# Layer 2's strips: one tile column of 64 rows a turn in place of 16 rows by 32 columns

## The chip, the cores and the metric

The kernel runs on one core of one Trainium2 chip. The metric is the device time of one execution in microseconds (us). TensorE (PE, with PEld for its weight loads), VectorE (DVE), ScalarE (ACT) and GpSimd (POOL) compute; SyncE (SP) issues every transfer between the chip's memory (HBM) and the on-chip memory. All arithmetic is in f32.

## The reference, cut to what matters

Sixteen images of 64 x 64 tokens with 256 channels pass through four residual layers, each fed by a group normalisation:

```
x = x + attention(gn(x))          # layer 0
x = x + gated_scan(gn(x))         # layer 1, ends in a batch norm over all images
x = x + involution3(gn(x))        # layer 2, 3x3 kernels made from x
x = x + involution7(gn(x))        # layer 3, 7x7 kernels made from x
```

The change concerns how the output of layer 2 reaches layer 3. Layer 3 multiplies 7x7 patches by weights that differ from token to token. Its patches are of the normalised tensor, so the mean of each channel's group is taken off first ("centred"); the scale is applied later. Tokens outside the image count as zero after centring.

## The kernel before, in words

**Three stages.** The first does layer 0 and the maps of layer 1 (to about 3420 us, layer 1's scan in it), the second (here stage B) the end of layer 1 and layer 2, the third (stage C, from about 6090 us) layer 3.

**Stage B** (from L899) is a loop over 152 turns, its order written by hand. An image has eight chunks of 512 tokens; in a turn the loop runs four jobs on chunks of different images, behind each other by the `LAG` of L1184. `end_of_layer1` (lag 0) makes `x2` from `x1` and the factors `pf`: DVE's two operations at L975, ACT, then POOL's two additions at L985. `projected` (lag 13) is PE and ACT work. The 3x3 involution (lag 21) is the DVE's heavy part: two products at L1107 of 4608 elements a partition and one sum at L1276; the other sum is made on POOL (L1120 in three steps, L1121), which DVE adds to at L1228. `turned` transposes the result `x3` (written as `x3_d`, token-major) to `c3` (written as `c3_d`, channel-major), and `norm3` finds the group means after an image's last chunk. `centred` (lag 32) is the job that the diff touches: it takes 512 tokens of `x3_d` into a tile `xc`, POOL subtracts the means at L880 into `cen`, and `cen` is written to the DRAM tensor `strips`.

**The tensor `strips`** is `[image, 4 quarters of 64 channels, 64 + 9 rows, 8 + 6 columns, 8 tile columns, 64 channels]`. Stage C works on tiles of 3 rows by 8 columns with a border of 3, so the 64 columns are kept as eight tile columns of 14, side by side; columns near a tile's edge are stored twice, once for its neighbour. A token's position inside the tile is u (0 to 7), its tile column t (0 to 7). For u from 5 to 7 there is a second copy for the next tile column, for u from 0 to 2 one for the previous.

**The job before:** job `rc` takes 16 rows (`part`) and half of the tile columns (`th`), so 16 x 32 tokens, by four loads with u slowest on the 128 partitions (p = 16 u + r). It writes, for each of the four quarters, three transfers: all eight u, then the two borders of three u each: 12 transfers.

**The transfers** all stand in SP's program, so SP's queue has this order in a turn: loads of the next turn (`x2p`, `x2r`, `x1` twice, `pf` twice), then the stores collected in the turn before (`x2`, the 12 strips, `x3` twice, `c3` twice), then the four loads of `xc`: 27 transfers. L942 is the line of the loads, L1213 that of the stores, L1281 that of the stores left at the end.

**The last image** is centred in stage C. Stage C has 704 turns `n` (16 images, 4 quarters, 11 pairs of tile rows). Each loads two sets of patches for the turn n + 4 (`xw`, L1413), every second one the residual (`rx`, L1433) and an output store (L1527); every third loads `c3` for the turn n + 2 (L1313), from which the next image's 7x7 weights start with the matmul at L1346. PE makes weight matrices (L1379) and applies them (L1445). Eight times, at turns n = 44 k + 1, `xc` is loaded (L1521), POOL centres in the turn after, and the 12 stores follow four a turn (L1523). `xc` and `cen` use two of the six buffers of `xw` here.

Of the kernel before, what the change touches and what calls it, by code (L numbers as in the profile page):

```python
# [15 lines left out]
P = 128  # L16
C = 256
HW = 64
# [10 lines left out]
TR, TC = 3, 8  # L29
NTR, NTC = 22, HW // TC  # L30
# [6 lines left out]
def network(ctx: ExitStack, tc: tile.TileContext, a: dict, out: bass.AP):  # L37
    nc = tc.nc
    NI = a["x"].shape[0]
# [45 lines left out]
    x3_d = dram.tile([NI, NT, C], F32, tag="x3_d", name="x3_d")  # L85
    c3_d = dram.tile([NI, P, 2, NT], F32, tag="c3_d", name="c3_d")
    strips = dram.tile([NI, 4, HW + 9, TC + 6, NTC, 64], F32, tag="strips", name="strips")
# [92 lines left out]
    with ExitStack() as st:  # L180
# [12 lines left out]
        for v in (wo[:, 0], wo[:, 1], bout):  # L193
            mean = small.tile([P, 1], F32, tag="wmean", name="wmean")
# [20 lines left out]
        def load(kind, i, ch):  # L215

            tag = {"xin": "xin", "xn": "xn"}.get(kind, "x1")
            t = wk.tile([P, 2, CT], F32, tag=tag, name=kind, bufs=4 if tag == "x1" else 2)
            src = a["x"][i, ch]
            if kind == "xm":  # L220
                src = x1_d[i, :, :, ch * CT : (ch + 1) * CT].rearrange("h p t -> p h t")
            nc.sync.dma_start(out=t, in_=src)
            loaded[kind, i, ch] = t
# [293 lines left out]
        def jobs(n):  # L517
            m, t = divmod(n, NCH)
            i, hf = divmod(m, 2)
            d = n - LAST  # L520

            def at(k):
                return 0 <= k < NI

            todo = []
            if at(i):
                todo.append(("q", i, hf, t))
            if hf == 0:
                if at(i + 1):
                    todo.append(("xin", i + 1, t))  # L530
            elif at(i - 1) and d < 0:
                todo.append(("x1", i - 1, t))
            if 6 <= d < 10:
                todo += [("x1", NI - 1, 2 * d - 12 + k) for k in range(2)]

            if at(i - 2) and (t >= 2 if hf == 0 else t < 2):
                todo.append(("xm", i - 2, (t - 2) % NCH))
            if 12 <= d < 16:
                todo += [("xm", NI - 1, 2 * d - 24 + k) for k in range(2)]
            return todo  # L540
# [24 lines left out]
        for n in range(LAST + 16):  # L565
            m, t = divmod(n, NCH)
# [64 lines left out]
    with ExitStack() as st:  # L631
# [24 lines left out]
        with tc.tile_pool(name="s_conv", bufs=1) as pcv:  # L656
# [4 lines left out]
                out=lsa.rearrange("p i j c -> p (i j c)"), in_=a["lsa_w"].partition_broadcast(P)  # L661
# [27 lines left out]
        for n in range(10):  # L689
            delta, c = n // 2, n % 2  # L690
# [28 lines left out]
        with tc.manual_schedule():  # L719
            steps = [(ch, g) for ch in range(NCH) for g in range(NG)]  # L720
            rows, ins, hsts = {}, {}, {}
# [23 lines left out]
            for n, (ch, g) in enumerate(steps):  # L745
# [18 lines left out]
                b, k = g * 8, min(8, NI - g * 8)  # L764
# [8 lines left out]
        n = NI * NCH  # L773
# [94 lines left out]
            )  # L868
        return lambda: nc.vector.tensor_copy(dst, pb[:, 0:C])

    def centred_from(i, rc):

        part, th = divmod(rc, 2)
        x3n = x3_d[i].rearrange("(r t u) c -> u r t c", t=NTC, u=TC)
        return [x3n[:, part * 16 : part * 16 + 16, th * 4 + t, :] for t in range(4)]

    def centred_strips(i, rc, xc, cen, mean):

        part, th = divmod(rc, 2)
        nc.gpsimd.tensor_tensor(  # L880
            cen.rearrange("p q t c -> p t q c"),
            xc.rearrange("p t (q c) -> p t q c", q=4),
            mean.rearrange("p (q c) -> p q c", q=4).unsqueeze(1).broadcast_to([P, 4, 4, 64]),
            ALU.subtract,
        )
        parts = []
        rows = slice(3 + 16 * part, 19 + 16 * part)
        for q in range(4):
            for u0, u1, w0, dt in ((0, TC, 3, 0), (TC - 3, TC, 0, 1), (0, 3, TC + 3, -1)):
                t0, t1 = max(0, th * 4 + dt), min(NTC, th * 4 + 4 + dt)  # L890
                s0 = t0 - th * 4 - dt
                parts.append((
                    strips[i, q, rows, w0 : w0 + u1 - u0, t0:t1, :].rearrange("r w t c -> w r (t c)"),
                    cen[16 * u0 : 16 * u1, q, s0 : s0 + t1 - t0, :].rearrange("p t c -> p (t c)"),
                ))
        return parts


    with ExitStack() as st:  # L899
# [58 lines left out]
            ))  # L958

        def load_centred(i, rc):  # L960
            load("xc", [P, 4, C], *(
                (lambda t, k=k: t[:, k], src) for k, src in enumerate(centred_from(i, rc))
            ))

        def end_of_layer1(i, rc):

# [205 lines left out]
        def centred(i, rc):  # L1172
            cen = wk.tile([P, 4, 4, 64], F32, tag="cen", name="cen")
            stores.extend(centred_strips(i, rc, taken("xc"), cen, gmb[i]))
# [29 lines left out]
        with tc.manual_schedule():  # L1204
            loads(0)
            ahead, made, ending = None, None, None
            for n in range(TURNS):
                end, proj, inv, cen = jobs(n)
# [6 lines left out]
                if nxt_cen:  # L1215
                    load_centred(*nxt_cen)
# [68 lines left out]
    with ExitStack() as st:  # L1285
# [6 lines left out]
        def cconst(name, shape, src=None):  # L1292
            t = pc.tile(shape, F32, tag=name, name=name)
            if src is not None:
                nc.sync.dma_start(out=t, in_=src)
            return t
# [110 lines left out]
        def load_patches(i, quarter, t):  # L1407

            xw = wk.tile([P, 2, NTC, 64], F32, tag="xw", name="xw", bufs=6)
            rows = strips[i, quarter].rearrange("r w t c -> (r w) (t c)")  # L1410
            for k in range(2):
                t0 = (t + k * NTT) * TR * (TC + 6)
                nc.sync.dma_start(  # L1413
                    out=xw[:, k].rearrange("p t c -> p (t c)"), in_=rows[t0 : t0 + P]
                )
            return xw
# [64 lines left out]
        mean = cconst("mean", [P, C])  # L1481
# [6 lines left out]
        gap = min(44, (4 * NTT * (NI - 1) - 4) // NCH)  # L1488
        for n, (i, quarter, t) in enumerate(turns):
            if quarter == t == 0:  # L1490

                pm = sm.tile([P, CT], F32, tag="sm", name="pm")
                for k in range(2):
                    for j in range(2):
                        nc.tensor.matmul(
                            pm[64 * k : 64 * k + 64, 2 * j : 2 * j + 2],
                            lhsT=ident[:, 64 * j : 64 * j + 64], rhs=rs3[:, i, :],
                            start=True, stop=True,
                        )
                msk = small.tile([P, 2, 2, 2], F32, tag="msk", name="msk")  # L1500
                nc.vector.tensor_tensor(
                    msk.rearrange("p j k g -> p (j k) g"),
                    pm[:, 0:4].unsqueeze(2).broadcast_to([P, 4, 2]),
                    gpar.unsqueeze(1).broadcast_to([P, 4, 2]),
                    ALU.mult,
                )
            if t == 0:
                making = iter(())
                if n + NTT < len(turns):
                    making = matrices(*turns[n + NTT][:2])  # L1510
            if n + 4 < len(turns):
                pats.append(load_patches(*turns[n + 4]))
            if t % 2 == 0:
                ex = wk.tile([P, 2, TR * HW], F32, tag="ex", name="ex", bufs=4)
                rx = res.pop(0)
            if n + 2 < len(turns) and turns[n + 2][2] % 2 == 0:
                res.append(load_residual(*turns[n + 2]))
            if n % gap == 1 and n // gap < NCH:
                xc = wk.tile([P, 4, C], F32, tag="xw", name="xc", bufs=6)
                for k, src in enumerate(centred_from(NI - 1, n // gap)):  # L1520
                    nc.sync.dma_start(out=xc[:, k], in_=src)  # L1521
            for dst, src in strip_stores[:4]:
                nc.sync.dma_start(out=dst, in_=src)  # L1523
            del strip_stores[:4]
            if done and done[0][0] == n:
                for dst, src in done.pop(0)[1]:
                    nc.sync.dma_start(out=dst, in_=src)  # L1527
            if n + 2 in features:
                cs[features[n + 2]] = load_reduced(*features[n + 2])
            involution7(i, quarter, t, wms[i, quarter], msk, pats.pop(0), ex[:, t % 2], rx[:, t % 2])  # L1530
            if n % gap == 2 and n // gap < NCH:
                cen = wk.tile([P, 4, 4, 64], F32, tag="xw", name="cen", bufs=6)
                strip_stores.extend(centred_strips(NI - 1, n // gap, xc, cen, mean))
            for _ in range(STEPS[t]):
                next(making, None)
            if n in features:
                tp, k = features[n]
                reduced(k, tp, cs.pop((tp, k)))
            if t == NTT - 1:
                next(making, None)  # L1540
                del wms[i, quarter]
            if t % 2 or t == NTT - 1:
                parts = halves(ex, out[i, quarter * 64 : quarter * 64 + 64], t - t % 2)
                done.append((n + 3, [(d, s) for s, d in parts]))
# [117 lines left out]
```

## Time and profile before

| | |
|---|---|
| median of 3 runs | 8457.71 us (8452.96 to 8464.74) |
| profiled execution | 8468.96 us, span 8467.2 us |
| busy: PE, PEld | 6869.9 us (81%), 5190.6 us (61%) |
| busy: DVE, ACT, POOL | 6077.2 us (72%), 4826.2 us (57%), 3076.3 us (36%) |
| transfers | 1695.64 MB, mean 200 GB/s |
| stage B, `xc` loads | 480 transfers of 128 KB (32 more in stage C) |
| stage B, strip stores | 1440 transfers of 36 to 128 KB (96 more in stage C) |
| POOL's L880 | 128 operations, 2.38 us each |

An instruction's row in a timeline gives its start and duration, its line and tiles (a digit in a name is dropped: `x_d` stands for `x1_d`, `x2_d` and `x3_d`, `x` for `x1`, `x2` and `x3`, `z<-x,ngm,pf` for the operation at L975), and in brackets the engine's idle time before it with what ended it.

### The profile page before, as it was taken

How to read it: one execution, taken by the hardware profiler on the slowest of the kernel's cores; microseconds unless marked ns; L12 is line 12 of the kernel's file. 1: busy time of each engine (PE TensorE's matmuls, PEld its weight loads, DVE VectorE, ACT ScalarE, POOL GpSimd, SP SyncE). 2: the span in 40 equal slices, each digit the busy share in tenths (PEclk: the TensorE clock that was granted, in tenths of full speed). 3: DMA queues.
4: the chain of work that ended last, by engine and by line, in shares of the span. 5: the costliest groups of instructions: out<-in, count | busy, mean ns of one | idle time of the engine just before them, and what ended most of it. 6: DMA issues, size and time to landing. Idle time of an engine off the chain costs nothing. (4 is left out here: it accounts for less than half of the span.)

```text
span 8467.2 us, 214899 instructions
## 1 busy us (share of the span) xinstructions
PE 6869.9 (81%) x88348; PEld 5190.6 (61%) x88348; DVE 6077.2 (72%) x7071; ACT 4826.2 (57%) x11136; POOL 3076.3 (36%) x2154
## 2 busy tenths in 40 slices
PE   7888888888888776487777777878588888888887
PEld 5666666666666552265555555555377777777776
DVE  6777787787777757499999999999644444444444
ACT  3555565555555437566666666665355555555554
POOL 1222222222222200367777777777511212111212
PEclk9999999999999868788899888889699999999999
DMA  7644443433333227757777777776578788888887
GB/s 223 188 139 135 135 140 131 151 130 135 132 115 120 95 74 258 229 187 238 239 241 238 239 239 239 239 236 210 189 227 252 247 250 256 254 259 251 258 258 235
DMA packets 1081767, 1695.64 MB, mean 200 GB/s; under 512 B 138833, under 2 KB 684962, under 8 KB 1079634
## 3 DMA queue, kind: packets, MB, share of 16 engines
q1 hardware_dynamic: 1080786, 1681.90, 61.4%
q8 instruction: 696, 11.40, 0.6%
q14 instruction: 285, 2.33, 0.1%
HBM read 1234.54 MB, written 469.76 MB: 201 GB/s over the span
## 5 line engine op out<-in xcount | busy, mean ns | idle before, releaser
L1107 DVE TENSOR_TENSOR pd<-xs,pw 128x4608 f32<-128x4608 f32 x256 | 1255.8, 4947 | 0.0
L1379 PE MATMUL pk<-rt,span 64*128 64x176 f32 x12288 | 1181.7, 329 | 54.7 <-issue 48.0
L1389 ACT ACTIVATE wm<-pk,spanb 128x176 f32<-128x176 f32 x2560 | 847.5, 425 | 565.4 <-PE pk L1379 562.1
L1465 POOL TENSOR_TENSOR ex<-ex,rx 128x192 f32<-128x192 f32 (+2 forms) x768 | 436.9, 570 | 1856.2 <-DVE ex L1458 1300.4
L1120 POOL TENSOR_TENSOR pd<-pd 128x2048 f32<-128x2048 f32 (+2 forms) x384 | 1071.1, 2789 | 92.0 <-DVE pd L1107 71.9
L1458 DVE SCALAR_TENSOR_TENSOR ex<-pa,msk,ex 128x192 f32<-128x192 f32 x704 | 294.2, 418 | 1054.9 <-ACT ex L1457 993.6
L1379 PEld LDWEIGHTS pk<-rt,span 64*128 64x128 f32 x12288 | 970.7, 192 | 128.5 <-issue 71.3
L1084 PE MATMUL pt<-ident,pad 128*128 128x128 f32 x4608 | 724.4, 318 | 347.8 <-ACT xs L1088 308.2
L292 PE MATMUL pkv<-wq,xn 128*128 128x256 f32 x4096 | 971.4, 383 | 13.0 <-ACT va L301 13.0
L375 POOL TENSOR_TENSOR qa<-qa,mq 128x1024 f32<-128x1024 f32 x256 | 507.4, 2004 | 1171.1 <-DVE mq L384 480.9
L1084 PEld LDWEIGHTS pt<-ident,pad 128*128 128x128 f32 x4608 | 606.5, 164 | 530.4 <-ACT xs L1088 354.0
L1445 PE MATMUL pa<-wm,xw 126*32 126x48 f32 x45056 | 756.2, 215 | 214.3 <-issue 191.8
L1394 DVE TENSOR_TENSOR wm<-pk,spanb 128x704 f32<-128x704 f32 x896 | 793.9, 888 | 184.6 <-PE pk L1379 182.2
L292 PEld LDWEIGHTS pkv<-wq,xn 128*128 128x128 f32 x4096 | 773.7, 192 | 226.3 <-issue 102.2
L1445 PEld LDWEIGHTS pa<-wm,xw 126*32 126x32 f32 x45056 | 624.7, 112 | 404.3 <-issue 353.4
L1038 PE MATMUL px<-x2p,wis 128*128 128x512 f32 x1024 | 525.2, 658 | 139.8 <-DVE gm L140 56.0
L1276 DVE TENSOR_REDUCE x<-pd 128x512 f32<-128x4608 f32 x128 | 633.5, 4949 | 1.9
L1088 ACT COPY xs<-pt 128x512 f32<-128x512 f32 x1152 | 596.0, 590 | 50.3 <-PE pt L1084 46.8
L280 PE MATMUL pq<-xn,wq 128*128 128x512 f32 x1024 | 531.3, 634 | 93.6 <-DVE xn L166 73.2
L423 PE MATMUL py<-wo,o 128*128 128x256 f32 x2048 | 533.0, 417 | 33.0 <-DVE maps L510 29.0
L423 PEld LDWEIGHTS py<-wo,o 128*128 128x128 f32 x2048 | 492.5, 311 | 67.9 <-issue 39.6
L1457 ACT ACTIVATE ex<-pa,msk 128x192 f32<-128x192 f32 x704 | 299.9, 426 | 398.3 <-PE pa L1445 200.7
(234 smaller groups left out, 11852.3 us busy)
## 6 DMA issues: line engine op xcount, KB each, us to landing
xw<-strips SPq DMA_DIRECT2D x1408, 256.0 KB
xn<-in_x SPq DMA_DIRECT2D x256, 512.0 KB
x_d<-x SPq DMA_DIRECT2D x256, 512.0 KB
xin<-in_x SPq DMA_DIRECT2D x128, 512.0 KB
x<-in_x SPq DMA_DIRECT2D x128, 512.0 KB
xm<-x_d SPq DMA_DIRECT2D x128, 512.0 KB
x<-x_d SPq DMA_DIRECT2D x128, 512.0 KB
x<-x_d SPq DMA_DIRECT2D x256, 256.0 KB
```

The lines of the kernel that those rows point to most:

```text
L280: nc.tensor.matmul(pq, lhsT=wq[:, h, f0 : f0 + P], rhs=xn[:, h], start=(h == 0), stop=(h == 1),)
L292: nc.tensor.matmul(pkv[:, q], lhsT=xn[:, h, q * P : (q + 1) * P], rhs=wq[:, h, f0 + P : f0 + 384], start=(h == 0), stop=(h == 1),)
L423: nc.tensor.matmul(py[:, q, :], lhsT=om[i, hf][:, :, ch * 4 + q], rhs=wo[:, hf, :], start=(hf == 0), stop=(hf == 1),)
L1084: nc.tensor.transpose(pt[:, k, h * P : (h + 1) * P], lines[:, h, rc * 4 + e + k, 2 * j : 2 * j + P], ident,)
L1088: nc.scalar.copy(xs[:, e : e + 2, j, :], pt)
L1107: nc.vector.tensor_tensor(pd.rearrange("p r (g f) k -> p r g f k", f=16), run, pw.rearrange("p r (g k) -> p r g k", k=9).unsqueeze(3).broa ...
L1120: nc.gpsimd.tensor_tensor(pd[..., 0:n], pd[..., 0:n], pd[..., n : 2 * n], ALU.add)
L1276: nc.vector.tensor_reduce(x3[:, :, P:C], pd1, AX.X, ALU.add)
L1379: nc.tensor.matmul(pkv[:, b, m], lhsT=span[half, first + gg, s0 : s0 + P], rhs=rto[half, o // 4 * 2 + m, :], start=True, stop=True,)
L1389: nc.scalar.activation(dst[:, m // 2, m % 2], pkv[:, m // 2, m % 2], AF.Identity, bias=spanb[:, g0 + m : g0 + m + 1],)
L1394: nc.vector.tensor_tensor(dst, pkv, spanb[:, g0 : g0 + 4].rearrange("p (b m) -> p b m", b=2).unsqueeze(3).broadcast_to([P, 2, 2, NTL]), AL ...
L1445: nc.tensor.matmul(pav[p0 : p0 + 32, :, tj * TC : (tj + 1) * TC].rearrange("c g (w v) -> c g w v", v=2), lhsT=xw[0:TILE_IN, k, tj, 32 * q ...
```

## The change

A job now takes one value of u: all 64 rows, all eight tile columns, 512 tokens again. It loads them in one transfer, with p = 2 r + th on the partitions, `th` being the half of the tile columns. POOL's operation has the same shape. For each copy of the column (one for u = 3 and 4, two for the others) it writes two transfers, one for each `th`, from every second partition and with all four quarters in one transfer: two transfers for u = 3 and 4 and four for the others, 28 for an image in place of 96. The bytes and the runs of 1 KB or 768 B that they consist of are the same. `centred_from` returns one source instead of four, and the two loads of it follow.

```diff
-    def centred_from(i, rc):
-        part, th = divmod(rc, 2)
-        x3n = x3_d[i].rearrange("(r t u) c -> u r t c", t=NTC, u=TC)
-        return [x3n[:, part * 16 : part * 16 + 16, th * 4 + t, :] for t in range(4)]
-    def centred_strips(i, rc, xc, cen, mean):
-        part, th = divmod(rc, 2)
+    def centred_from(i, u):
+        return x3_d[i].rearrange("(p t u) c -> u p t c", t=4, u=TC)[u]
+    def centred_strips(i, u, xc, cen, mean):
...
         parts = []
-        rows = slice(3 + 16 * part, 19 + 16 * part)
-        for q in range(4):
-            for u0, u1, w0, dt in ((0, TC, 3, 0), (TC - 3, TC, 0, 1), (0, 3, TC + 3, -1)):
+        copies = [(u + 3, 0)] + [(u - 5, 1)] * (u >= TC - 3) + [(u + TC + 3, -1)] * (u < 3)
+        for w, dt in copies:
+            for th in range(2):
                 t0, t1 = max(0, th * 4 + dt), min(NTC, th * 4 + 4 + dt)
                 s0 = t0 - th * 4 - dt
                 parts.append((
-                    strips[i, q, rows, w0 : w0 + u1 - u0, t0:t1, :].rearrange("r w t c -> w r (t c)"),
-                    cen[16 * u0 : 16 * u1, q, s0 : s0 + t1 - t0, :].rearrange("p t c -> p (t c)"),
+                    strips[i, :, 3 : 3 + HW, w, t0:t1, :].rearrange("q r t c -> r q (t c)"),
+                    cen[th:P:2, :, s0 : s0 + t1 - t0, :].rearrange("p q t c -> p q (t c)"),
                 ))
         return parts
...
         def load_centred(i, rc):
-            load("xc", [P, 4, C], *(
-                (lambda t, k=k: t[:, k], src) for k, src in enumerate(centred_from(i, rc))
-            ))
+            load("xc", [P, 4, C], (lambda t: t, centred_from(i, rc)))
...
-                for k, src in enumerate(centred_from(NI - 1, n // gap)):
-                    nc.sync.dma_start(out=xc[:, k], in_=src)
+                nc.sync.dma_start(out=xc, in_=centred_from(NI - 1, n // gap))
```

## The prediction

> **What bounds the kernel now.** The chain of work that ended last covers only the final microseconds, so I read the stretches one by one. Page first, then busy time by stretch, then SP's, GpSimd's (POOL) and VectorE's (DVE) timelines in one turn of stage B, then the waits of stage C. Busy time (stretch, its length, then PE, PEld, DVE, ACT, POOL with counts, clock, DMA share, GB/s), before SP fills up and after:
>
> ```profile
> 3736.00:3890.00 154.00, 122.65 (x667) 89.26 (x666) 151.36 (x84) 102.76 (x233) 116.35 (x58) 0.89 0.65 218
> 4208.00:4368.00 160.00, 123.06 (x665) 88.35 (x664) 154.60 (x83) 101.91 (x229) 123.39 (x59) 0.89 0.72 240
> ```
>
> Both hold eight turns. DVE looks full in both, yet the second takes longer for the same work. The timelines (start, duration, engine, operation, count, idle time before) say why:
>
> ```profile
> 4808.53 9.94 SPq L1213 DMA_DIRECT2D strips<-cen  x12
> 4818.57 1.28 SPq L1213 DMA_DIRECT2D x_d<-x  x2
> 4819.95 1.11 SPq L1213 DMA_DIRECT2D c_d<-c  x2
> 4821.11 2.63 SPq L942 DMA_DIRECT2D xc<-x_d  x4
> 4823.84 0.40 SPq L942 DMA_DIRECT2D x2p<-x_d  x1
> ...
> 4828.73 0.62 SPq L1213 DMA_DIRECT2D strips<-cen  x1
> ```
> ```profile
> 4819.60 1.97 POOL L1121 TENSOR_TENSOR x<-pd 128x512 f32<-128x512 f32 x1
> ...
> 4829.00 2.38 POOL L880 TENSOR_TENSOR cen<-xc,gmb 128x1024 f32<-128x1024 f32 x1 [4.51 <-DMA x2p<-x_d]
> ```
> ```profile
> 4818.48 1.58 DVE L975 SCALAR_TENSOR_TENSOR z<-x,ngm,pf 128x512 f32<-128x512 f32 x1
> 4820.10 2.02 DVE L975 SCALAR_TENSOR_TENSOR pf<-x,ngm,pf 128x512 f32<-128x512 f32 x1
> ```
>
> SP issues without pause: its lap from strips to strips, 20.2 us, is the turn. Summed over the 64 turns from 4208 to 5498, a turn of 20.15 us holds 16.6 of SP issuing 27 transfers, 1.5 in gaps and semaphore instructions (0.05 a transfer), and 2.1 waiting, mostly for a transfer issued eight before: in the trace's semaphore fields SP's transfers share eight completion semaphores in rotation. So `xc` is issued late, POOL stands 4.5 us before `cen` (3.4 on average), its sums of products end late, and DVE's L975 meets POOL's L1121: 1.58 and 2.02 us where it takes 0.75 when POOL is quiet. DVE's busy time hides a wait.
>
> Stage C, waits of PE while the last image is centred (6160 to 7380), then at the stage's start (6060 to 6140):
>
> ```profile
> PE pr L1346 <- DMA c<-c_d: 52.9, 8, 7.2
> ```
> ```profile
> PE pm L1331 <- DVE wr L1325: 27.0, 1, 27.0
> ```
>
> The first wait does not occur in the rest of stage C. SP issues 4.45 transfers per 3.22 us turn, 2.73 us of issue plus 0.22 of gaps: 92% full without any centring.
>
> **What the Trainium skill says.** "DMA: Bandwidth & Descriptors", section "Why a DMA increments its semaphore by 16 and not by 1": a transfer uses the largest k up to 16 that divides the slowest dimension of both sides, on the lowest-numbered engines. The trace agrees: the semaphores show 3 data landings for a halo store (dims 3 by 16), 8 for a main store or an `xc` part, 16 for the x3 store; and of `x2p`, issued at 4803.60, half the engines land by 4807.31, the last at 4810.03. Section "Issuing engines are not separate DMA queues" calls issue time usually small beside the transfer; here it fills the turn, and the measurement decides. "SBUF — State Buffer", section "Who interferes with whom": a DVE instruction with two SBUF inputs contends with a GpSimd instruction that reads SBUF, the first holding the port; L975 above agrees, ending 0.55 us after POOL's operation.
>
> **The change part by part.** Moved bytes and the POOL operation (2.38 us, same shape) stay.
>
> *Load of xc.* Four transfers of 0.63 us (2.5) become one of 512 rows of 1 KB. Not shown before; nearest are the x1 load (256 rows, 0.52) and the c3 store (0.50): I take 0.55, between 0.4 and, if issue time followed the rows, 2.5.
>
> *Strip stores.* Twelve a turn (4 of 0.63, 8 of 0.70: 8.1 us) become 28 per image over eight turns, 3.5. Nearest is the x3 store, also every second partition with four 1 KB rows: 0.64, so 2.2 us; bounds 0.6 and 1.4 each (2.1 to 4.9).
>
> *Sum for SP in stage B.* The other eleven transfers keep 5.9; 5.9+0.55+2.2+0.8 of gaps (15.5 transfers)=9.5 us a turn. Even both upper ends and today's waits give 5.9+2.5+4.9+0.8+2.1=16.2, under DVE's 18.4 below. SP stops setting the turn.
>
> *What binds next.* DVE. Eight turns before centring starts: 18.4 us each (3589.6 to 3736.7). The next eight hold centring but SP is not yet behind: 19.13 (3736.7 to 3889.7; POOL never waits for `cen` there, L975 stays at 0.75, one turn is unusually long). I take 19.0. Turns 16 to 103 (3889.7 to 5657.2) take 20.09: 88×1.09=96 us. Of the later turns only the first few are behind, 6 us. **Stage B: −102**; bounds −60 and −135.
>
> *Waits.* `xc` now needs all 64 rows of the image instead of 16, so its first load follows the last x3 store; that store is issued one SP block earlier, cover enough. Strips still wait once for `cen`; behind them on SP queue the x3 and c3 stores and the next `xc`, with half a turn of slack. If strips had to wait for each other, see the second rival.
>
> *End of stage B.* From 6062 (last c3) to 6092.7 SP issues leftover strips, stores, `xc`, strips, strips; PE and DVE wait 27 us for constants queued behind. Afterwards: c3 and x3 stores at 6062 to 6064, `xc`, landing and `cen` to about 6070, four strips to 6073. **−19**, bounds −10 and −20.
>
> *Stage C.* Eight times, 4 loads and 12 stores (4×0.65+12×0.68+16×0.05=11.6 us of SP) become 1 and 3.5 (3.2 us with gaps). The eight groups of eleven turns in which this happens sum to 353 us, the same groups of the other eight images to 287: 66 us lost, 8.3 each. Prefetch of two turns covers about 11.6−8.3=3.3 us, so 3.2 nearly disappears; I leave 1.4 each. **−55**, bounds −25 and −66. The two of six `xw` buffers held by `xc` and `cen` come free sooner; costed at nothing.
>
> Sum: −102−19−55=−176. The profiled execution took 8468.96 us (span 8467.2 and 1.8 around it): 8293. The median of the runs, 8457.7, is 0.13% below it: about **8282**.
>
> **The rivals.**
>
> *Forecast, SP relieved:* 0.82. For: SP's lap equals the turn; turns with slack are faster. Against: DVE already reads 97% busy, so each gain is small.
>
> *Faster, but little:* strips wait for each other, or the 512-row load issues slowly. A store is issued at 4818.57 and lands at 4822.39, 3.8 us; 3.5 such waits instead of 0.69 give 5.9+0.55+13.3+0.8=20.6 us, today's turn. Against: today's strips also interleave in the same rows, and are issued 0.7 us apart. Then stages B and C keep their time, 8458 ± 25. If only half the ring waits remain, 8380. Together 0.12.
>
> *Slower:* the rows now lie 32 KB (loads) and 28 KB (stores) apart. The DMA page ("Latency and other measured facts") tells of loss at row pitches of large powers of two, from 512 KB; the quarters lie 2.09 MB apart, not a power of two. Price: DMA is busy 0.72×20.1=14.5 us a turn; the moved 1.4 of 4.8 MB is 4.2 of it. Every doubling of those rows adds 4.2 us; from 2.3 times the present cost the engines fill the turn, at 3 times a turn is 22.9 us, +2.8×88=+246: 8700. Against: the c3 store has this 32 KB pitch and follows 0.8 us behind its neighbour, x1 at 16 KB moves 256 KB in 0.72 us. 0.06.
>
> **How the numbers follow.** A measurement of this kernel can tell about 0.2%, 17 us, from no change. Bounds of the parts: −60−10−25=−95 gives 8363; −135−20−66=−221 gives 8237. With the half case the range is 8225 to 8385, leaving out about 0.17. Faster 0.82 plus 0.07 of the small-gain case: 0.89; same 0.05; slower 0.06.
>
> **What would show it.** In the profile after: SP with pauses of several us in each turn of stage B; one `xc` transfer and 2 to 4 strips; POOL's idle time before L880 down from 3.4 us to under 0.5; L975 near 0.75; turns at 18.6 to 19.2; stage C starting its constants within 12 us of the last c3 store; PE's wait for `c<-c_d` gone from the first half of stage C. I am wrong if SP is relieved and the turn stays at 20 us (then DVE or the DMA engines held it), or if `xc` or strips take over 2 us to issue.

## The result and the profile after

| | before | after |
|---|---|---|
| median, in one comparison | 8461.06 us (4 runs, 8452.96 to 8464.74) | 8346.40 us (4 runs, 8335.11 to 8355.00) |
| ratio, 95% interval | | 0.9865 (0.9848 to 0.9882) |
| profiled execution | 8468.96 us, span 8467.2 us | 8343.11 us, span 8341.3 us |

The change makes the kernel 115 us faster. The forecast was 176 us faster: right in direction, and too large by half. Cutting both profiled executions at the same instructions (the starts of DVE's sums at L1276 for the turns of stage B, then those of ACT's first and last operation at L1457 for stage C) shows where the time came from:

| stretch | before | after | difference | forecast |
|---|---|---|---|---|
| up to DVE's first sum of stage B | 3589.6 | 3576.5 | -13.1 | 0 |
| turns 0 to 15 | 300.2 | 300.3 | +0.1 | 0 |
| turns 16 to 103 | 1767.5 (20.09 a turn) | 1707.2 (19.40 a turn) | -60.3 | -96 |
| turns 104 to 126 | 396.0 | 395.8 | -0.2 | -6 |
| last turn to stage C | 101.3 | 86.6 | -14.7 | -19 |
| stage C | 2306.1 | 2269.1 | -37.0 | -55 |

The first row is no effect of the change: no instruction of it differs, and over the fourteen profiled executions of this study it lay between 3560.3 and 3593.1 us. The 112 us of the other rows are the change.

The line numbers of the kernel after are a few lower: L1107 became L1102, L975 L970, L985 L980, L1121 L1116, L880 L877, L942 L939, L1213 L1208, L1346 L1341, and in stage C L1379 L1374 and L1445 L1440. The same operations are meant. In experiments that add or drop lines the numbers shift by a few more.

Busy time by stretch first, in the columns of before, for the same two groups of eight turns:

```profile
3724.00:3877.00 153.00, 122.34 (x665) 89.31 (x664) 150.41 (x83) 101.80 (x231) 115.46 (x57) 0.89 0.68 229
4184.00:4338.00 154.00, 122.14 (x667) 87.33 (x666) 151.64 (x84) 101.81 (x232) 120.18 (x59) 0.91 0.74 250
```

The second stretch took 160 us before and takes 154 now, nearly as little as the first: the slowing down once SP is behind is gone. But DVE is still 98% busy at 19.2 us a turn. The SP timeline of one turn shows the relief:

```profile
4807.70 0.33 SPq L939 DMA_DIRECT2D x2p<-x_d  x1
4808.09 0.42 SPq L939 DMA_DIRECT2D x2r<-x_d  x1
4808.61 0.89 SPq L939 DMA_DIRECT2D x<-x_d  x2
4809.59 0.91 SPq L939 DMA_DIRECT2D pf<-fac_d  x2
4810.55 0.42 SPq L1208 DMA_DIRECT2D x_d<-x  x1
4811.07 3.77 SPq L1208 DMA_DIRECT2D strips<-cen  x4
4814.95 1.28 SPq L1208 DMA_DIRECT2D x_d<-x  x2
4816.69 1.67 SPq L1208 DMA_DIRECT2D c_d<-c  x2
4818.66 0.56 SPq L939 DMA_DIRECT2D xc<-x_d  x1
4827.30 0.33 SPq L939 DMA_DIRECT2D x2p<-x_d  x1
```

From 4819.22 to 4827.30 SP issues nothing: 8 us of pause. Over the 64 turns from 4184 to 5430 a turn holds 9.13 us of issuing 15.5 transfers, 0.85 of gaps and about 9.3 of waiting. `xc` is one transfer of 0.56 us here (0.64 on average). A strip store is not 0.64 us: four in a row took 3.77, and the mean of the two shapes is 0.88 and 0.91.

POOL no longer waits for `xc`: its idle time before `cen` fell from 3.4 us to 0.0 in all 64 turns. What that does to DVE is seen when both timelines of this turn are laid beside each other. DVE:

```profile
4811.65 0.75 DVE L970 SCALAR_TENSOR_TENSOR z<-x,ngm,pf 128x512 f32<-128x512 f32 x1
4812.44 0.75 DVE L970 SCALAR_TENSOR_TENSOR pf<-x,ngm,pf 128x512 f32<-128x512 f32 x1
...
4813.50 1.20 DVE L121 TENSOR_TENSOR mom<-gn_mv,ngm 128x2 f32<-128x2 f32 x1
4814.74 1.20 DVE L122 TENSOR_TENSOR mom<-mom 128x2 f32<-128x2 f32 x1
4815.97 2.27 DVE L123 SCALAR_TENSOR_TENSOR gn_mv<-mom 128x2 f32<-128x2 f32 x1
```

and POOL:

```profile
4813.42 1.27 POOL L980 TENSOR_TENSOR x<-z,x 128x512 f32<-128x512 f32 x1 [1.97 <-ACT z L976]
4814.65 1.27 POOL L980 TENSOR_TENSOR x<-pf,x 128x512 f32<-128x512 f32 x1
4815.88 2.35 POOL L877 TENSOR_TENSOR cen<-xc,gmb 128x1024 f32<-128x1024 f32 x1
```

The two operations at L970 are back at 0.75 us, as forecast. Behind them stand small ones that the prediction never mentions: L93 to L148 are the helpers of the group norms, which make a mean and a variance out of sums, two elements a partition. Each needs 0.16 us alone. L121, L122 and L123 start within 0.1 us of a POOL operation and end with it: 1.20, 1.20 and 2.27 us. So `cen`, which used to come 3.4 us later, now meets L123. In the groups of DVE over 64 turns (name, shape, count, busy us, mean ns, idle before), first before:

```profile
L121 DVE TENSOR_TENSOR mom<-gn_mv,ngm 128x2 f32<-128x2 f32 x16 | 19.1, 1194 | 0.6
...
L122 DVE TENSOR_TENSOR mom<-mom 128x2 f32<-128x2 f32 x16 | 5.7, 355 | 0.6
...
L123 DVE SCALAR_TENSOR_TENSOR gn_mv<-mom 128x2 f32<-128x2 f32 x16 | 2.6, 161 | 0.6
```

and after:

```profile
L123 DVE SCALAR_TENSOR_TENSOR gn_mv<-mom 128x2 f32<-128x2 f32 x16 | 35.4, 2210 | 0.5
L122 DVE TENSOR_TENSOR mom<-mom 128x2 f32<-128x2 f32 x16 | 19.2, 1201 | 0.6
L121 DVE TENSOR_TENSOR mom<-gn_mv,ngm 128x2 f32<-128x2 f32 x16 | 18.2, 1138 | 0.6
```

L123 went from 0.16 to 2.21 us. All operations from L93 to L148 together went from 8.47 to 12.81 us per eight turns, +0.54 a turn. The two at L970 fell from 1.285 to 0.809 us, -0.95 a turn. More than half of what L970 gave back was taken by operations that compute 256 numbers.

Stage C, waits of PE (total us, times, longest) at the end of stage B (5985 to 6045), then from 6060 to 7300, while the last image is centred:

```profile
PE pm L1326 <- DVE wr L1320: 11.9, 1, 11.9
```
```profile
PE pr L1341 <- DMA c<-c_d: 25.6, 7, 6.9
```

The first was 27.0 us and fell by 15.1, as its stretch did by 14.7. The second was 52.9 and was to be gone; it fell by 27 us, in a stage that became 37 shorter (that the two need not go together is seen in e13).

### The profile page after: what moved, and what is told of

The parts are those of the page before. It is cut to its first block, busy times and chain, and to the rows that moved or that the text cites. A ratio compares the mean times of both kernels' runs of the same rounds, so it can differ in the third digit from the quotient of the medians.

```text
span 8341.3 us, 213203 instructions
## 1 busy us (share of the span) xinstructions
PE 6856.8 (82%) x88348; PEld 5190.5 (62%) x88348; DVE 6037.4 (72%) x7071; ACT 4816.7 (58%) x11136; POOL 3044.7 (37%) x2154
## 5 line engine op out<-in xcount | busy, mean ns | idle before, releaser
L1102 DVE TENSOR_TENSOR pd<-xs,pw 128x4608 f32<-128x4608 f32 x256 | 1255.6, 4945 | 0.0
L1374 PE MATMUL pk<-rt,span 64*128 64x176 f32 x12288 | 1180.3, 328 | 51.6 <-issue 46.0
L1384 ACT ACTIVATE wm<-pk,spanb 128x176 f32<-128x176 f32 x2560 | 845.8, 425 | 564.3 <-PE pk L1374 561.3
L1460 POOL TENSOR_TENSOR ex<-ex,rx 128x192 f32<-128x192 f32 (+2 forms) x768 | 437.0, 570 | 1832.5 <-DVE ex L1453 1356.5
L1374 PEld LDWEIGHTS pk<-rt,span 64*128 64x128 f32 x12288 | 969.9, 191 | 129.3 <-issue 73.0
L1440 PE MATMUL pa<-wm,xw 126*32 126x48 f32 x45056 | 754.9, 214 | 216.0 <-issue 201.2
L1440 PEld LDWEIGHTS pa<-wm,xw 126*32 126x32 f32 x45056 | 622.7, 111 | 400.7 <-issue 353.7
L1033 PE MATMUL px<-x2p,wis 128*128 128x512 f32 x1024 | 497.0, 627 | 76.4 <-DVE ngm L142 45.8
L1452 ACT ACTIVATE ex<-pa,msk 128x192 f32<-128x192 f32 x704 | 299.6, 426 | 391.0 <-PE pa L1440 193.8
```

Source lines behind the costliest of these rows:

```text
L1102: nc.vector.tensor_tensor(pd.rearrange("p r (g f) k -> p r g f k", f=16), run, pw.rearrange("p r (g k) -> p r g k", k=9).unsqueeze(3).broa ...
L1374: nc.tensor.matmul(pkv[:, b, m], lhsT=span[half, first + gg, s0 : s0 + P], rhs=rto[half, o // 4 * 2 + m, :], start=True, stop=True,)
L1384: nc.scalar.activation(dst[:, m // 2, m % 2], pkv[:, m // 2, m % 2], AF.Identity, bias=spanb[:, g0 + m : g0 + m + 1],)
L1440: nc.tensor.matmul(pav[p0 : p0 + 32, :, tj * TC : (tj + 1) * TC].rearrange("c g (w v) -> c g w v", v=2), lhsT=xw[0:TILE_IN, k, tj, 32 * q ...
```

## The experiments

All experiments are compared with the kernel before on the same chip. "Small operations" are those at L93 to L148; "the turn" is the mean of turns 16 to 103; "an eight" is eight turns, one image. "The eight groups" are those of eleven turns of stage C in which the last image is centred. They take 353.3 us before and 310.9 after; the same groups of the other eight images 286.6 and 285.1. So the loss by centring fell from 67 to 26 us. It is a coarse measure: the other four executions with stage C as changed (e2, e4, e5, e11) gave 17, 36, 39 and 22 us, so that a difference of some 10 us in it says nothing.

### The new layout with as many transfers as the old: e1_many

The first question was whether the gain is SP's number of transfers or that the new transfers spread more evenly over the DMA engines (a halo store before used 3 of them). This kernel keeps the new layout, with rows in multiples of 16 in every transfer, but splits them by quarters:

```diff
-                parts.append((
-                    strips[i, :, 3 : 3 + HW, w, t0:t1, :].rearrange("q r t c -> r q (t c)"),
-                    cen[th:P:2, :, s0 : s0 + t1 - t0, :].rearrange("p q t c -> p q (t c)"),
-                ))
+                for q in range(4):
+                    parts.append((
+                        strips[i, q, 3 : 3 + HW, w, t0:t1, :].rearrange("r t c -> r (t c)"),
+                        cen[th:P:2, q, s0 : s0 + t1 - t0, :].rearrange("p t c -> p (t c)"),
+                    ))
...
-            load("xc", [P, 4, C], (lambda t: t, centred_from(i, rc)))
+            load("xc", [P, 4, C], *(
+                (lambda t, k=k: t[:, k], centred_from(i, rc)[:, k]) for k in range(4)
+            ))
```

(and the same four loads in stage C).

> The changed kernel with as many transfers as before: the new layout on the partitions, but the load of xc in four transfers and each strip store cut into its four quarters (14 stores a turn on average; 29 transfers a turn in place of 27 before and 15.5 after). All of them run on 16 engines. If the number of transfers that SP issues is what held stage B (theory S), SP needs 5.9 + 4x0.63 + 14x0.64 + 1.5 of gaps + about 2 of waits = 21 us a turn, so a turn takes 20 to 21 us and the kernel 8440 to 8540 us. If the uneven spread over the DMA engines held it (theory E), a turn stays at 19.4 us and the kernel at 8340 to 8390 us.

Measured: 8476.05 us, ratio 1.0032 (1.0024 to 1.0041); the turn 20.15 us. SP issues 16.25 us of it for 29 transfers and waits 2.5. Its timeline:

```profile
4813.41 6.93 SPq L1211 DMA_DIRECT2D strips<-cen  x8
4820.44 1.74 SPq L1211 DMA_DIRECT2D x_d<-x  x2
4822.27 1.09 SPq L1211 DMA_DIRECT2D c_d<-c  x2
4823.42 2.20 SPq L940 DMA_DIRECT2D xc<-x_d  x4
4825.72 0.38 SPq L940 DMA_DIRECT2D x2p<-x_d  x1
```

No pause, as before. The eight groups of stage C lose as well: 370.2 us. So the gain is that there are fewer transfers; the layout by itself, with two transfers more than before, brings nothing.

### The new kernel with two uneven stores more: e2_skew

The converse: two stores a turn of 192 KB with a slowest dimension of 3 are added, into a tensor that nobody reads.

```diff
+    spare = dram.tile([NI, NCH, 2, 16, 4, 1024], F32, tag="spare", name="spare")
...
             stores.extend(centred_strips(i, rc, taken("xc"), cen, gmb[i]))
+            for k in range(2):
+                stores.append((
+                    spare[i, rc, k, :, 0:3].rearrange("r w c -> w r c"),
+                    cen[48 * k : 48 * k + 48].rearrange("p q t c -> p (q t c)"),
+                ))
```

> The changed kernel with the uneven spread put back: in each turn of stage B that centres, two more stores of 192 KB go from cen to a scratch tensor, their slowest dimension 3, so on three engines, 128 KB more for each of these (the old halo stores put 112 KB there). SP issues 17.5 transfers a turn, about 10.5 us with gaps. Theory S: the turn stays at 19.4 us, the kernel at 8335 to 8365 us. Theory E: the turn goes back towards 20 us, the kernel to 8390 to 8460 us.

Measured: 8359.64 us, ratio 0.9884 (0.9864 to 0.9904), which overlaps the interval of the changed kernel; the turn 19.45 us. SP now issues 12.7 us for 17.5 transfers and still waits 5.7. Of the 3.6 us more of issue only 1.5 are the two stores' own: transfers behind them took longer to issue than in the changed kernel (`xc` 1.27 us for 0.64, a `c3` store 1.10 for 0.51). The turns pay nothing measurable for either, as long as SP has pauses. Where SP has none, at the end of stage B, it shows: the constants of stage C are first issued at 6014.90 us in place of 6002.90, and PE waits 27.3 us for them in place of 11.9.

### The order of DVE's program: e3_before_order and e4_after_order

In both kernels DVE's program has the two operations at L970 ahead of the small ones. L970 feeds ACT and, through it, POOL's L980, and `cen` is next in POOL's program; the small ones then fall just under these. Two lines moved put the small ones first:

```diff
                 squares, ending = ending, end_of_layer1(*end) if end else None
-                if ending:
-                    next(ending)
                 step()
                 for c in begun:
                     next(c)
                 chains.extend(begun)
                 begun.clear()
+                if ending:
+                    next(ending)
```

The edit was made in the kernel before (e3) and in the changed kernel (e4).

> The kernel before with one change of DVE's order in stage B: the small operations of the group norms (the step of running chains and the first part of a new one) come ahead of the two operations at L975 instead of behind them, so they meet a quiet POOL. Theory S: SP's lap of 20.1 us still sets the turn, and the kernel gains at most 20 us: 8435 to 8465 us. If DVE's waits for the port set the turn by themselves (theory D), it gains what DVE saves, 0.4 us a turn and more, 35 to 80 us: 8380 to 8425 us.

> The changed kernel with the same change of DVE's order. After the change two of eight turns take 22.6 us, because three small operations of a group norm wait for three POOL operations in a row, the last one cen, which is now early. If this is where the missing part of the forecast gain went, the three take 0.16 us each, these turns fall to about 19 us, L975 stays at 0.75, and the kernel goes to 8250 to 8290 us. Rival: the waits are only shifted, to L975 or to the group norm's later steps, and the kernel stays at 8330 to 8350 us.

Measured:

| | old order | small operations first |
|---|---|---|
| kernel before | 8449.87 us, turn 20.09 | 8445.25 us, turn 20.13; ratio 0.9989 (0.9979 to 0.9998) |
| changed kernel | 8346.40 us, turn 19.40; ratio 0.9865 | 8215.65 us, turn 18.20; ratio 0.9715 (0.9694 to 0.9736) |

DVE of e4, at the same place of a turn:

```profile
4740.39 0.16 DVE L121 TENSOR_TENSOR mom<-gn_mv,ngm 128x2 f32<-128x2 f32 x1
4740.58 0.16 DVE L122 TENSOR_TENSOR mom<-mom 128x2 f32<-128x2 f32 x1
4740.78 0.16 DVE L123 SCALAR_TENSOR_TENSOR gn_mv<-mom 128x2 f32<-128x2 f32 x1
4740.99 0.75 DVE L970 SCALAR_TENSOR_TENSOR z<-x,ngm,pf 128x512 f32<-128x512 f32 x1
4741.78 0.75 DVE L970 SCALAR_TENSOR_TENSOR pf<-x,ngm,pf 128x512 f32<-128x512 f32 x1
```

Per eight turns the operations from L93 to L148 take 3.64 us in place of 12.81: 1.15 us a turn less, and over the same 64 turns the turn fell by 1.23 (19.47 to 18.24). That is the floor that the changed kernel missed.

The row of e3 says more: with SP behind, the same edit brings 5 us in all. Its first turns, before SP is behind, do get shorter (turns 0 to 15: 289.2 us in place of 300.2). After that a turn takes 20.13, with SP as full as before (16.4 us of issuing, 2.2 of waiting). e3 and e4 run the same program on DVE; with 27 transfers a turn takes 20.13 us, with 15.5 it takes 18.20. So before the change SP set the turn, and after it DVE does. But e3 does not show a DVE that was spared work and gained nothing by it. With POOL late, the small operations meet it at other places (L122 takes 1.21 us on average, L148 1.20): they take 10.42 us per eight turns, where the kernel before has 8.47, and DVE's busy time is the same (19.4 us a turn). The edit pays only where `cen` is on time, and each repair is worth little without the other: -5 and -115 alone, -234 together, each in its own comparison with the kernel before.

### Taking a wait off the head of SP's queue: e5_after_late

SP waits about 9.3 us a turn in the changed kernel, 7.4 of it in one place (waits of SP, 4184 to 5430: total, times, longest):

```profile
SPq L939 <- PE px L1033: 475.5, 56, 14.5
```

That is the load of `x2p`, whose buffer PE has not yet read out, with the stores of `x2`, strips and all else behind it. In 40 of the turns from 16 to 103 there is a rhythm of 19.64 us in which one turn of eight takes 20.07 with DVE short of input. So `x2p` was moved to the end of the block:

```diff
-            end, proj, _, _ = jobs(n)
-            if proj:
-                load("x2p", [P, 2, CT], (lambda t: t, x2_d[proj[0], proj[1]]))
+            end = jobs(n)[0]
...
+                nxt_proj = jobs(n + 1)[1]
+                if nxt_proj:
+                    load("x2p", [P, 2, CT], (lambda t: t, x2_d[nxt_proj[0], nxt_proj[1]]))
```

> The changed kernel with the load of x2p moved in SP's block from ahead of the stores to behind them and behind the xc load (it fetches what the next turn's block would have fetched). Theory 'a wait at the head of SP's queue costs part of each triple of turns': SP no longer stands (14.4 us in the turn looked at) on the buffer of x2p with the stores and the pf and x1 loads behind it; the turns of 18.8, 18.8 and 20.1 us in the middle of stage B lose the 20.1, about -18 us in the whole: 8320 to 8335. Rival 'DVE's meetings with cen set these turns, not the queue': no change, 8340 to 8355, and the turn from 16 to 103 stays at 19.4 us.

Measured: 8336.83 us, ratio 0.9862 (0.9840 to 0.9883), the changed kernel's. The theory's 20.07 us turns are gone and nothing is gained: nearly all eights now take 19.36 in place of a mix of 19.22 and 19.64. The wait has a new owner, the next load in the block:

```profile
SPq L939 <- PE lo L1095: 524.0, 64, 12.0
```

SP's wait is slack. It is as long as the turn leaves it, wherever it stands in the queue.

### Stage C with the old transfers: e7_c_old

Stage B is the changed one; the last image is loaded by four and stored by twelve transfers a step, as before.

```diff
-                nc.sync.dma_start(out=xc, in_=centred_from(NI - 1, n // gap))
+                for k, src in enumerate(centred_from_old(NI - 1, n // gap)):
+                    nc.sync.dma_start(out=xc[:, k], in_=src)
...
-                strip_stores.extend(centred_strips(NI - 1, n // gap, xc, cen, mean))
+                strip_stores.extend(centred_strips_old(NI - 1, n // gap, xc, cen, mean))
```

> The changed kernel in stage B; in stage C the last image is loaded and stored as in the kernel before (four loads, twelve stores a step). Theory 'stage C's gain is SP's number of transfers there': the eight groups of eleven turns that hold centring lose about 67 us against the same groups of other images, as before, in place of 26, so 8380 to 8390; stage B and the gap between the stages stay (19.4 us a turn). Rival 'stage C gained for another reason, such as what stage B leaves behind': 8335 to 8355.

Measured: 8388.03 us, ratio 0.9924 (0.9904 to 0.9944). Stage B (19.47 us a turn) and the end of stage B (85.4) are the changed kernel's; stage C takes 2302.3 us as before, and the eight groups 353.7. PE waits for `c` as before (6060 to 7300):

```profile
PE pr L1368 <- DMA c<-c_d: 54.3, 8, 8.2
```

So the share of stage C is shown by itself: against the changed kernel 33 us in the stage's length, 43 in the eight groups and 42 in the median. It comes from the transfers of the last image.

### What is left in stage C: e8_spread, e10_act, e13_order_pool

The groups still lose some 26 us. The turn with the longest wait for `c` (6.9 us) follows four strip stores in a row, 2.96 us of SP, with six loads of patches behind. In e8 one strip store a turn is issued:

```diff
-            for dst, src in strip_stores[:4]:
+            for dst, src in strip_stores[:1]:
                 nc.sync.dma_start(out=dst, in_=src)
-            del strip_stores[:4]
+            del strip_stores[:1]
```

> The changed kernel with one strip store a turn in stage C in place of up to four. Theory 'the rest of stage C's loss, 26 us in eight groups, comes from about 3 us of strip stores in one turn, behind which the patches are late': the loss falls to about 10, so -15: 8325 to 8335. Rival 'SP is over 90% full there anyway, so that spreading moves nothing, since the backlog is the same': no change, 8340 to 8355.

Measured: 8324.77 us, ratio 0.9852 (0.9828 to 0.9876), which can't be told from the changed kernel; the eight groups 318.4, PE's wait for `c` 23.9 us (6100 to 7300; the changed kernel 22.7 there). A burst of four stores alone is not to blame. In e10 the strip stores leave SP altogether:

```diff
-                nc.sync.dma_start(out=dst, in_=src)
+                nc.scalar.dma_start(out=dst, in_=src)
```

> The changed kernel; in stage C the strip stores are issued on ACT's queue instead of SP's, the same transfers at the same place of the program. The strip stores one a turn in place of four did not lower stage C's loss (26 us in the changed kernel, 35 with one a turn). Theory 'SP has no room there, so every microsecond of issue that centring adds, some 3 us each time, comes back as a wait for c or for patches, however it is spread': with the stores off SP only the xc load of 0.6 us is left, the eight groups lose under 10 us, PE's wait for c falls from 23 us to under 8: about -18 us against the changed kernel on the same chip, 8315 to 8330. Rival 'it is the traffic of the strips in the DMA engines, not the queue': the loss stays at 20 to 30 us and the time with the changed kernel's. Rival 'ACT, which evicts in each turn, is held by the issue': the loss stays or grows, and ACT's idle time before L1452 shows it.

Measured: 8375.33 us, ratio 0.9879 (0.9852 to 0.9905), where the changed kernel took 8339.65 on the same chip (e11); stage C 2295.9 us and the eight groups 344.9. Waits of PE, then of ACT (6060 to 7300):

```profile
PE pk L1374 <- ACT wm L1384: 50.3, 11, 9.2
...
PE pr L1341 <- DMA c<-c_d: 5.1, 3, 3.8
```
```profile
ACT wm L1384 <- POOL ex L1460: 63.4, 8, 11.6
```

The wait for `c` is nearly gone, so it had come from the stores in SP's queue. In its place ACT stands eight times, up to 11.6 us, because a strip store ahead of its evictions waits for POOL's `cen`; PE then waits for the weight matrices that ACT evicts. (The view names POOL's L1460, the addition of the residual; it is `cen` that ends these waits: at 7124.01 us a `cen` ends, and ACT issues the store at 7124.04.) This is nearest to the third of the outcomes put down beforehand, but ACT is held by the wait for `cen` and not by issuing, and at L1384 rather than at L1452.

In e13 POOL issues the stores itself, behind its own `cen`, in e4's order of DVE (the edit is the last one with `nc.gpsimd`).

> As the kernel with DVE's small operations ahead of L970, and in stage C the strip stores are issued by POOL, behind its own centring, in place of SP. On ACT's queue the stores made ACT stand up to 11.6 us on POOL's centring, which itself stood 9.4 us on the landing of xc in the turn looked at; PE's wait for c fell from 22.7 to 5.1 us, but 50.3 us of waits of PE for ACT's weight matrices came. POOL waits for nobody more, since its centring stands ahead of the stores in its own queue. Theory 'SP's issue time is what costs': the eight groups lose under 15 us in place of 36, 8190 to 8205. Rival 'POOL's standing on xc, with the additions at L1460 queued behind it, costs as much': the loss stays at 25 to 40, 8210 to 8225, and PE's or ACT's waits behind L1460 show it. Rival 'issuing from POOL is slow': over 8225, with gaps on POOL ahead of L1460.

Measured: 8222.58 us, ratio 0.9723 (0.9702 to 0.9744), where e4 has 0.9715. Waits of PE, 6060 to 7300 ("issue" stands where the profile shows nothing that was waited for):

```profile
PE pk L1374 <- issue: 45.1, 44, 2.5
PE pa L1440 <- DMA xw<-strips: 9.7, 7, 3.0
PE pr L1341 <- DMA c<-c_d: 3.8, 2, 3.0
```

The wait for `c` fell from e4's 25.4 to 3.8 us, ACT did not stand for `cen` as in e10, and stage C still takes 2260.2 us (e4: 2260.0). The eight groups take 307.8 us (e4: 316.1), within what they vary by. PE idles about as long as in e4 but in other places: the first line of the view is 25.4 us in e4, the second 3.9. So the wait for `c` is where part of the stage's remaining loss shows, and taking it away did not shorten the stage. What makes the loss, POOL's standing on `xc` (9.4 us in the turn looked at in the changed kernel, with L1460 behind it), the traffic or something else, was not settled.

### The pieces together, and the changed kernel again: e9_best, e12_order_act, e11_again

> The changed kernel with three edits: DVE's small operations at the end of layer 1 ahead of L970 in its program (the order of the run that measured 8215.65), x2p loaded last in SP's block, and one strip store a turn in stage C. If each of the last two acts as its theory says and the effects add up: 8180 to 8195. If neither acts: 8210 to 8225. If with the new order the wait for x2p is the only one left in SP's queue, the turn falls from 18.2 to about 18.0.

Measured: 8241.16 us, ratio 0.9752 (0.9729 to 0.9776): e4's order with e5's and e8's edits is not better than e4 alone. It looks rather worse, though the two intervals still touch. Its turn is 18.31 us; one turn in eight often takes 21.16, with DVE's wait at L1021 for PE at up to 3.4 us (20.2 us in 64 turns; in e4 up to 1.1, and 8.8).

> The changed kernel with DVE's small operations of the end of layer 1 ahead of L970 (8215.65 when it was measured) and stage C's strip stores on ACT's queue. If the two act alone and add up: 8190 to 8200, with the eight groups of stage C losing under 10 us in place of 36. If the stores' queue is not what costs in stage C: 8210 to 8225.

Measured: 8248.33 us, ratio 0.9734 (0.9713 to 0.9755); the eight groups 331.1. As in e10, ACT stands for `cen` (37.6 us in seven waits), and its queue is the wrong place.

> The changed kernel once more, on the chip of the others, so that small differences to it can be read: 8335 to 8355. In stage B the turns 16 to 103 have taken 1692 to 1714 us with the same instructions in four executions; if that is one of several rhythms that an execution falls into, it is again in this span.

Measured: 8339.65 us, ratio 0.9848 (0.9830 to 0.9866), against the kernel before on its own chip. Turns 16 to 103 take 1704.4 us, the eight groups 313.6: the main rows of the table at the top repeat themselves.

The best kernel of the study is e4, 8215.65 us; e13 can't be told apart from it.

## Why the prediction was right, and where it was too large

The measured 8346 us lies in the range given, and the mechanism held. But all three parts came out smaller than forecast: -60 for -102, -14.7 for -19, -37 for -55.

**The bound.** "SP's lap equals the turn" held: with the number of transfers given back (e1) the turn is 20.15, with SP relieved it falls, and the same program on DVE takes 20.13 with the old transfers (e3) and 18.20 with the new (e4).

**SP's sum.** 9.5 us a turn forecast, 9.13 of issue and 0.85 of gaps, so 9.98, measured. Two terms were off against each other: a strip store takes 0.88 to 0.91 us where 0.64 was taken from the x3 store (3.5 of them: 3.1 us, not 2.2), and the other eleven transfers take 5.4, not 5.9. (The first strip store of a row did take 0.59 us, those behind it 1.0 on average; why is not shown.) The `xc` load was 0.64 for 0.55. None mattered, since SP is left with 9 us of waiting; e2 adds 3.6 us of issue without effect on the turn.

**What binds next: the step that failed.** The floor was taken from turns 8 to 15 of the kernel before, 19.13 us, "one turn is unusually long", and rounded down to 19.0. That turn, 22.64 us, was not an accident but the rule. DVE of the kernel before in it:

```profile
3801.51 1.21 DVE L121 TENSOR_TENSOR mom<-gn_mv,ngm 128x2 f32<-128x2 f32 x1
3802.75 1.20 DVE L122 TENSOR_TENSOR mom<-mom 128x2 f32<-128x2 f32 x1
3803.98 2.27 DVE L123 SCALAR_TENSOR_TENSOR gn_mv<-mom 128x2 f32<-128x2 f32 x1
```

Here `cen` was on time (POOL's L880 starts at 3803.89) and L123 met it, for 2.27 us. Two turns of each eight hold such a chain. In turns 8 to 15 only one of the two was hit by `cen`, because centring starts between them: the other, before its start, took 20.52; in the changed kernel it takes 22.6 as well in nearly every eight from turn 16 on. These 2.1 us more in one turn of eight (L123's 2.27 in place of 0.16) add 0.26 a turn: 19.13 and 0.26 are 19.39, and 19.40 was measured. Of the 0.40 a turn by which the forecast floor was too low, 0.26 are thus the second turn and 0.13 the rounding. (Single eights take 19.1 to 19.4 a turn, and 19.64 in one rhythm.) So the size was to be read in the trace of before: its undisturbed stretch showed the very collision that a timely `cen` makes permanent. The prediction named the rule, from the Trainium skill's page "SBUF — State Buffer", section "Who interferes with whom", and applied it to L975 alone. That section says that the one that comes first keeps the shared port for its whole instruction (in its words on the two-port modes); the trace agrees, and for an operation of 0.16 us this wait is nearly all of its time. So the turns 16 to 103 gave -60 in place of -96, just the end that the bounds of stage B gave.

**Later turns.** -6 forecast, -0.2 measured: turns 104 to 126 took the same time before.

**End of stage B.** -19 forecast, -14.7 measured; PE's wait fell from 27.0 to 11.9. The constants are first issued at 6002.90, 14 us after the last `c` of stage B is ready (5988.9) and not 11. SP stood for the last `cen` (from the timelines of SP and POOL):

```profile
5992.77 0.72 SPq L939 DMA_DIRECT2D xc<-x_d  x1
5993.58 3.30 SPq L1208 DMA_DIRECT2D strips<-cen  x4
6000.21 2.59 SPq L1276 DMA_DIRECT2D strips<-cen  x4
```
```profile
5997.85 2.34 POOL L877 TENSOR_TENSOR cen<-xc,gmb 128x1024 f32<-128x1024 f32 x1 [1.17 <-issue]
```

Its `xc` was issued at 5992.77, behind four strips and the x3 and c3 stores, and by the trace's semaphore fields it landed at 5997.64; POOL was free from 5996.68. So the chain of store, load, landing and `cen`, put at 8 us behind the last `c`, took 11.3. That the constants start within 12 us of the last c3 store held (5991.54 to 6002.90, 11.4 us).

**Stage C.** -55 forecast, -37.0 measured, shown apart by e7. The groups' loss fell from 67 to 26 us; 11 was forecast. The term that failed is "prefetch covers about 3.3 us, so 3.2 nearly disappears": the loss is 3.2 us a step, about what centring still adds to SP (four stores 2.96, `xc` 0.58). But e13 took the stores from SP and the stage got no shorter, so SP's issue is not the whole account. The cause of the rest is open.

**The waits.** That `xc` now needs all 64 rows of its image cost nothing: POOL's idle time before `cen` is 0.0.

**The rivals.** Strips that wait for each other, or a slow load, would have left SP full; it pauses. Row pitch: the turn's DMA work did not grow to fill it; with 250 GB/s in the second stretch, above the 240 of before, the engines carry the same bytes in less time.

## What to carry to other kernels

When one engine stops being late, look at what its work will now land on: take the undisturbed stretch of the old trace, and explain its longest turn before calling it an accident. Where DVE and POOL work in turns, put DVE's tiny operations at a place where POOL is idle: what they cost is set by how many there are and by the length of the POOL operation that each one meets, not by their own size (here 9 us per eight turns, removed by moving two lines). A wait at the head of a queue that has pauses is slack: e5 moved it and gained nothing. And a wait that a view lists is not what its removal brings: e13 took PE's wait for `c` away, and the stage stayed as long.

## What the runs showed of the hardware

- An operation of DVE on 128x2 numbers took 0.16 us alone and 2.27 us beside POOL's `cen` of 2.35 us: it started 0.09 us after POOL's operation and ended with it.
- The issue of a strip store took from 0.58 to 1.5 us on SP in the changed kernel, mean 0.89, median 0.80. Splitting each into four cost more in the whole: 14 quarter stores took 8.17 us a turn (e1), the 3.5 whole ones 3.12.
- The changed kernel runs stage B in several rhythms, such as 19.2, 19.36 or 19.64 us a turn, each kept for several eights. Which one it falls into differs between executions of the same instructions: turns 16 to 103 took 1692.5 to 1713.7 us in five executions of the same stage B.
